# The sums of squares of a local-attention projection in a PSUM bank of their own

## The chip, the cores and the metric

The kernel runs on one core of a Trainium2 chip. The core has a matmul engine (TensorE, "PE" in the profile, with weight loads listed as PEld), a vector engine (VectorE, DVE), a scalar engine (ScalarE, ACT), a general engine (GpSimd, POOL) and SyncE (SP), which issues the DMAs here. Each engine works through its own list of instructions in order, and waits on semaphores for the others. Matmul results are written to PSUM, which the kernel divides into eight banks of 128 x 512 fp32 numbers. The metric is the time of one execution on the device in microseconds (us).

## The reference, cut to what matters

Two blocks, L0 and L1, follow each other on a batch of 2 with 2048 tokens of 128 numbers. Each block has an attention part and a "local model". The change lies in the local models: L0's has 6 layers with 16 heads and a window of 32, L1's has 2 layers with 8 heads and a window of 64; a head has 64 numbers. L1's linear attention lies between them. A layer of a local model computes this:

```python
def shift_token(x):
    t1, t2 = jnp.split(x, 2, axis=-1)
    t2 = jnp.pad(t2, ((0, 0), (1, 0), (0, 0)))[:, :-1]
    return jnp.concatenate([t1, t2], axis=-1)

def l2norm(t):
    return t / jnp.clip(jnp.linalg.norm(t, axis=-1, keepdims=True), 1e-12)

h = shift_token(x)
q, k, v = jnp.split(h @ wqkv, 3, axis=-1)      # then split into heads
q = l2norm(q) * qs
k = l2norm(k) * ksc
q, k = rotary_xpos(q, k)                       # t*cos*scale + rotate_half(t)*sin*scale; k with 1/scale
o = local_attention(q, k, v)                   # each window of queries sees its own and the last window
x = x + o @ wo
h = shift_token(x)
h = (h - mean) / sqrt(var + 1e-05) * lg + lb
a, g = jnp.split(h @ w1 + b1, 2, axis=-1)
x = x + (a * gelu(g)) @ w2 + b2
```

The norm inside `l2norm` needs, for each token and head, the sum of 64 squares and its reciprocal root.

## The kernel before, in words

A first stage computes L0's attention. Then `local_models` runs both local models in one loop. It works on tiles of 128 tokens: 16 tiles for each of 2 batches and each layer, 192 tiles for the first model and 64 for the second. The loop is a software pipeline: in one round it projects tile j, turns the rows of tile j-1 and computes its values, and does scores, softmax, mixing and the output of still earlier tiles.

For one tile these steps matter:

- `project` (L871 to L904) multiplies 128 tokens by 1024 columns of the weights into `pq` (`ps_qk`), a wide pair of PSUM banks. ACT squares it to `sq` (L873). DVE multiplies it by two tables, for the rotation, into `r` (L881) and `t` (L886), and POOL adds the two (L892). The first model needs two such units for a tile, half 0 and half 1, for its 2048 columns of queries and keys; the second needs one.
- After the last unit, DVE sums the squares by head (L897) and takes the reciprocal root in nine small steps (`rsqrt_quick`, L167 to L180). Their scratch, at most 128 columns, lies in `pq`. POOL multiplies `r` by the root (L904).
- `turn` (L936) transposes `r`, four transposes to a bank, into queries and keys (four banks a tile in the first model, two in the second).
- `values` (L955) projects the values, `scores` opens with a mask matmul (L986, two per tile, called M here) and adds the products (L995); DVE takes the maximum (L1003) and subtracts it (L1005), ACT takes the exponential (L1012), DVE sums (L1019), POOL scales (L1021).
- `keys_first_` (L1030) transposes the weights, `mix` (L1048) multiplies them with the values, `project_out` (L1065) projects the result (`ps_y`), and DVE adds it to the state (L1071).
- `feed_forward` works on four tiles at a time. Its steps (L1096, L1105 to L1110, L1128, L1131, L1148 twice, L1173) are put into a list, and each round of the loop takes two of them.

PSUM is split into two pools: `wide` hands out two pairs of banks in turn, for scores, projections and parts of the linear attention; `bank` hands out four single banks in turn, for everything else. An allocation waits until the last reader of the bank that it gets is done.

The order of instructions on each engine is not the order of the text. A scheduler in the build works from estimated durations and decides it, and with it which bank an allocation gets, and so which wait stands before which instruction. Once built, the order is fixed.

Of the kernel before, what the change touches and what calls it, by code (L numbers as in the profile page):

```python
# [72 lines left out]
def tile_kernel(ctx: ExitStack, tc: tile.TileContext, a: dict, out: bass.AP):  # L73
# [27 lines left out]
    def bc(ap, shape):  # L101
        return ap.to_broadcast(list(shape))
# [59 lines left out]
    def rsqrt_quick(scr, n, pool):  # L162

        x, xm, h, p = scr
        nc.vector.tensor_scalar(xm, x, 1e-24, None, ALU.max)  # L167
        y = pool.tile([128, n], F32, name="rq_g")
        nc.vector.tensor_scalar(
            y.bitcast(I32), xm.bitcast(I32), -0.5, RSQ_SEED, ALU.mult, ALU.add  # L170
        )
        nc.vector.tensor_tensor(p, xm, y, ALU.mult)
        hs_ = pool.tile([128, n], F32, name="rq_h")
        nc.vector.tensor_tensor(hs_, p, y, ALU.mult)
        nc.vector.tensor_tensor(h, p, y, ALU.mult)
        nc.vector.scalar_tensor_tensor(p, h, RSQ_A[0], hs_, ALU.add, ALU.mult)
        for c in RSQ_A[1:3]:
            nc.vector.scalar_tensor_tensor(p, p, c, hs_, ALU.add, ALU.mult)
        r = pool.tile([128, n], F32, name="rq_y", bufs=2)
        nc.vector.scalar_tensor_tensor(r, p, RSQ_A[3], y, ALU.add, ALU.mult)  # L180
        return r
# [526 lines left out]
    def local_models(mA, mB, hs0):  # L708
# [3 lines left out]
        wk = ctx2.enter_context(tc.tile_pool(name="f_k", bufs=1))  # L712
# [4 lines left out]
        def wide(name):  # L717

            return psA.tile([128, 1024], F32, tag="A", name=f"ps_{name}")

        def bank(name):
            return psT.tile([128, 512], F32, tag="T", name=f"ps_{name}")
# [139 lines left out]
        def project(i, u):  # L862
            g, b, t = tiles[i]
            m, _ = layers[g]
            H, units = m.H, m.units
            tb = tabs[g, t]
            hw = hs[0][:, b, t * 128:(t + 1) * 128]
            pq = wide("qk")
            for j in range(2):
                js = slice(512 * j, 512 * j + 512)  # L870
                nc.tensor.matmul(pq[:, js], lhsT=hw, rhs=wts[g, u][:, js], start=True, stop=True)  # L871
            sq = wk.tile([128, 1024], F32, name="sq", bufs=2)
            nc.scalar.activation(sq, pq, AF.Square)  # L873
            r = wk.tile([128, 1024], F32, name=f"r{u}", bufs=2)
            t2 = wk.tile([128, 1024], F32, name="t2", bufs=1)
            same = units[u][0][0] == units[u][1][0]
            for e in range(1) if same else range(2):
                s = units[u][e][0]
                hn = 16 if same else 8
                es = slice(512 * e, 512 * e + 64 * hn)  # L880
                nc.vector.tensor_tensor(  # L881
                    r[:, es].rearrange("p (h d) -> p h d", d=DH),
                    pq[:, es].rearrange("p (h d) -> p h d", d=DH),
                    bc(tb[:, 0, s].unsqueeze(1), (128, hn, DH)), ALU.mult,
                )
                nc.vector.tensor_tensor(  # L886
                    t2[:, es].rearrange("p (h s d) -> p h s d", s=2, d=32),
                    pq[:, es].rearrange("p (h s d) -> p h s d", s=2, d=32)[:, :, ::-1, :],
                    bc(tb[:, 1, s].rearrange("p (s d) -> p s d", s=2).unsqueeze(1),
                       (128, hn, 2, 32)), ALU.mult,  # L890
                )
            nc.gpsimd.tensor_tensor(r, r, t2, ALU.add)  # L892
            st[i]["r", u], st[i]["sq", u] = r, sq
            if u == len(units) - 1:

                for v in range(len(units)):
                    nc.vector.tensor_reduce(  # L897
                        pq[:, 16 * v:16 * v + 16],
                        st[i].pop(("sq", v)).rearrange("p (h d) -> p h d", d=DH), AX.X, ALU.add,
                    )  # L900
                y = rsqrt_quick([pq[:, k * 32:k * 32 + 2 * H] for k in range(4)], 2 * H, wk)
                for v in range(len(units)):
                    rv = st[i]["r", v].rearrange("p (h d) -> p h d", d=DH)
                    nc.gpsimd.tensor_tensor(  # L904
                        rv, rv, bc(y[:, 16 * v:16 * v + 16].unsqueeze(2), (128, 16, DH)), ALU.mult
                    )
# [554 lines left out]
        for i in range(-3, n):  # L1461
# [7 lines left out]
            if j < n:  # L1469
                g, b, t = tiles[j]  # L1470
                jj = j % per
                nu = len(layers[g][0].units)
                more = g < last
                if g == second and t % 4 == 0:
                    while (b, t // 4) not in ready:
                        lstep()
                if nu == 2:
                    project(j, 0)
                if more and jj == 4:
                    load_proj(g + 1, 0)  # L1480
                if more and jj == 6 and g + 1 == second:
                    models[1].consts()
                if jj == 6 and g == second - 1:
                    linear_consts()
                if more and jj == 8:
                    factors(g + 1)
                    if 2 == 2:
                        load_out(g + 1)
                if more and jj == 18:
                    load_ff(g + 1)  # L1490
                if more and jj == 22:
                    fold_ff(g + 1)
                if nu == 2 and more and jj == per - 1:
                    load_proj(g + 1, 1)
                lstep()
# [5 lines left out]
            if j < n:  # L1501
                project(j, nu - 1)
                if nu == 2 and more and jj == per - 1 and g + 1 < second:
                    load_proj(g + 1, 2)
                if nu == 1 and more and jj == per - 1:
                    load_proj(g + 1, 1)
                if b == B - 1 and j + 1 < n:
                    tables(*tiles[j + 1][::2])
# [93 lines left out]
```

## Time and profile before

| quantity | value |
|---|---|
| time, median of 3 runs | 4991.75 us (4983.2 to 4993.75) |
| the profiled execution's own time | 4992.08 us |
| its span, first to last instruction | 4990.3 us |
| busy: PE, DVE, ACT, POOL | 4522.4, 3949.9, 2641.9, 2783.4 us |
| granted TensorE clock, mean | 0.956 of full |
| first projection of the first model | at 572.7 us |
| first projection of the second model | at 3976.6 us |
| PE busy, 1500 to 1750 us (first model) | 240.2 of 250 us, clock 0.99 |
| PE busy, 4500 to 4750 us (second model) | 220.3 of 250 us, clock 0.95 |

A line of a group or of the timeline names the engine, the line of the kernel, the operation, the tile that is written and those that are read. "idle before <- X" is the time for which the engine stood still before the instruction, and what released it. The end of a matmul is modelled, so that neighbouring matmuls can overlap by some 0.15 us in the timeline.

### The profile page before, as it was taken

Reading aid. Unit: us, or ns where it says so; the run is one execution under the profiler, and the core shown is the slowest. Engines: PE = TensorE matmul, PEld = TensorE weight load, DVE = VectorE, ACT = ScalarE, POOL = GpSimd, SP = SyncE. Lnnn points to the kernel's source line nnn. Section 1 sums busy time; section 2 is a strip of 40 time slices with the busy share of each in tenths; the row PEclk is TensorE's granted clock in tenths of the full one; section 3 lists DMA queues with packets and bytes.
Section 4 is the critical chain, followed back from the end, with each engine's and each line's share of the span. In section 5 each row is a group of like instructions: output and inputs, shape, how many; then the busy total and the mean of one; then the engine's idle time right before and its main releaser. Section 6 shows DMA issues by size and latency. Waiting matters only on the chain.

```text
span 4990.3 us, 166474 instructions
## 1 busy us (share of the span) xinstructions
PE 4522.4 (91%) x73028; PEld 3080.9 (62%) x73058; DVE 3949.9 (79%) x6840; ACT 2641.9 (53%) x4207; POOL 2783.4 (56%) x1666
## 2 busy tenths in 40 slices
PE   5667799999999999999999999999999998989887
PEld 3445566666666666666666666666666665555554
DVE  6993488888887888888888888888877777778776
ACT  3223355555555555555555555555555555555554
POOL 3332366666666666666666666666555544455552
PEclk8778899999999999999999999999999999999999
DMA  2000222223222322232222322232221211111111
GB/s 77 1 1 25 84 68 67 64 72 78 68 64 63 84 71 64 64 82 72 65 70 61 80 67 64 66 82 68 55 58 49 63 45 40 40 46 40 50 48 41
DMA packets 222468, 295.32 MB, mean 59 GB/s; under 512 B 75656, under 2 KB 95408, under 8 KB 221744
## 3 DMA queue, kind: packets, MB, share of 16 engines
q1 hardware_dynamic: 221744, 284.67, 22.1%
q8 instruction: 576, 9.44, 0.8%
q14 instruction: 148, 1.21, 0.1%
HBM read 40.98 MB, written 10.75 MB: 10 GB/s over the span
## 4 chain that ended last, share of the span: by engine, by line
PE 47%; DVE 25%; ACT 7%; POOL 6%; issue 4%; DMA 1%; SPq 0%; POOLq 0%; DVEq 0%; ACTq 0%
PE ps_qk L871 11%; PE ps_o L1048 5%; PE ps_f L1148 5%; DVE ps_qk L897 5%; PE ps_v L955 5%; DVE t L886 5%; PE ps_turn L936 4%; POOL r L892 4%; PE ps_y L1065 4%; PE ps_s L995 3%; DVE r L881 3%; PE ps_fy L1173 3%; DVE rs L1019 2%; ACT sq L873 2%; PE ps_pT L1030 2%
## 5 line engine op out<-in xcount | busy, mean ns | idle before, releaser
L892 POOL TENSOR_TENSOR r<-r,t 128x1024 f32<-128x1024 f32 x448 | 1061.8, 2370 | 926.2 <-DVE t L886 814.6
L904 POOL TENSOR_TENSOR r<-r,rq_y 128x1024 f32<-128x1024 f32 x448 | 844.5, 1903 | 521.8 <-DVE rq_y L180 498.9
L873 ACT ACTIVATE sq<-ps_qk 128x1024 f32<-128x1024 f32 x448 | 461.0, 1029 | 1091.5 <-PE ps_qk L871 1026.4
L871 PE MATMUL ps_qk<-wp,hs 128*128 128x512 f32 x1792 | 894.9, 622 | 110.0 <-DVE rq_y L180 82.6
L881 DVE TENSOR_TENSOR r<-ps_qk,tb 128x1024 f32<-128x1024 f32 (+1 forms) x512 | 550.9, 1076 | 215.2 <-ACT sq L873 200.9
L1048 PEld LDWEIGHTS ps_o<-pT,v 64*64 64x64 f32 (+1 forms) x26624 | 479.4, 136 | 309.5 <-ACT pT L1031 162.4
L886 DVE TENSOR_TENSOR t<-ps_qk,tb 128x1024 f32<-128x1024 f32 (+1 forms) x512 | 554.5, 1083 | 145.5 <-POOL r L892 145.0
L1021 POOL TENSOR_TENSOR sm<-sm,rs 128x1024 f32<-128x1024 f32 x256 | 487.9, 1906 | 255.5 <-DVE rs L1020 172.7
L1048 PE MATMUL ps_o<-pT,v 64*64 64x32 f32 (+1 forms) x26624 | 532.1, 221 | 36.5 <-ACT pT L1031 19.9
L897 DVE TENSOR_REDUCE ps_qk<-sq 128x16 f32<-128x1024 f32 x448 | 549.2, 1226 | 12.0
L871 PEld LDWEIGHTS ps_qk<-wp,hs 128*128 128x128 f32 x1792 | 310.5, 193 | 367.6 <-issue 236.5
L936 PEld LDWEIGHTS ps_turn<-ident,r 128*128 128x128 f32 x3584 | 413.1, 144 | 157.0 <-issue 98.2
L936 PE MATMUL ps_turn<-ident,r 128*128 128x128 f32 x3584 | 450.1, 278 | 40.4 <-POOL r L904 36.9
L955 PE MATMUL ps_v<-wp,hs 128*128 128x512 f32 x896 | 482.2, 640 | 1.1 <-ACT oT L1054 0.8
L1065 PEld LDWEIGHTS ps_y<-oT,wo 128*128 128x128 f32 x3584 | 432.1, 193 | 48.3 <-issue 43.0
L1065 PE MATMUL ps_y<-oT,wo 128*128 128x128 f32 x3584 | 448.5, 277 | 1.7 <-ACT oT L1054 1.5
L1003 DVE TENSOR_REDUCE mx<-ps_s 128x16 f32<-128x1024 f32 (+1 forms) x256 | 312.5, 1221 | 101.5 <-PE ps_s L995 99.6
L1054 ACT COPY oT<-ps_o 128x512 f32<-128x512 f32 x448 | 243.8, 588 | 276.0 <-PE ps_o L1048 275.2
L995 PE MATMUL ps_s<-kT,qT 64*32 64x64 f32 (+1 forms) x26624 | 384.1, 231 | 0.3 <-issue 0.3
L995 PEld LDWEIGHTS ps_s<-kT,qT 64*32 64x32 f32 (+1 forms) x26624 | 331.0, 108 | 63.1 <-issue 49.4
L1148 PE MATMUL ps_f<-fx,w 128*128 128x512 f32 (+1 forms) x768 | 364.5, 612 | 2.3 <-DVE fx L1131 1.9
L1019 DVE TENSOR_REDUCE rs<-sm 128x16 f32<-128x1024 f32 (+1 forms) x256 | 310.6, 1213 | 62.3 <-ACT sm L1012 61.2
(265 smaller groups left out, 6860.3 us busy)
## 6 DMA issues: line engine op xcount, KB each, us to landing
v<-vn SPq DMA_DIRECT2D x1276, 128.0 KB
v<-vn SPq DMA_DIRECT2D x744, 64.0 KB
v<-vn SPq DMA_DIRECT2D x64, 256.0 KB
wp<-in_L_ffn_Wqkv SPq DMA_DIRECT2D x20, 512.0 KB
xD<-xb SPq DMA_DIRECT2D x24, 256.0 KB
xb<-xD SPq DMA_DIRECT2D x24, 256.0 KB
cs<-in_cos SPq DMA_DIRECT2D x128, 32.0 KB
cs<-in_sin SPq DMA_DIRECT2D x128, 32.0 KB
```

The lines of the kernel that those rows point to most:

```text
L871: nc.tensor.matmul(pq[:, js], lhsT=hw, rhs=wts[g, u][:, js], start=True, stop=True)
L881: nc.vector.tensor_tensor(r[:, es].rearrange("p (h d) -> p h d", d=DH), pq[:, es].rearrange("p (h d) -> p h d", d=DH), bc(tb[:, 0, s].unsq ...
L886: nc.vector.tensor_tensor(t2[:, es].rearrange("p (h s d) -> p h s d", s=2, d=32), pq[:, es].rearrange("p (h s d) -> p h s d", s=2, d=32)[: ...
L892: nc.gpsimd.tensor_tensor(r, r, t2, ALU.add)
L897: nc.vector.tensor_reduce(pq[:, 16 * v:16 * v + 16], st[i].pop(("sq", v)).rearrange("p (h d) -> p h d", d=DH), AX.X, ALU.add,)
L904: nc.gpsimd.tensor_tensor(rv, rv, bc(y[:, 16 * v:16 * v + 16].unsqueeze(2), (128, 16, DH)), ALU.mult)
L936: nc.tensor.transpose(p[:, c * 128:(c + 1) * 128], r[:, cs], ident)
L955: nc.tensor.matmul(p, lhsT=hw, rhs=wv, start=True, stop=True)
L995: nc.tensor.matmul(sp[W * w:W * w + W, c0:c0 + 2 * W], lhsT=qT[64 * q:64 * q + 64, cc, W * w:W * w + W], rhs=kT[64 * q:64 * q + 64, cc, W ...
L1048: nc.tensor.matmul(po[s][64 * q:64 * q + 64, 128 * c + W * w:128 * c + W * w + W], lhsT=v2[kp, w, co:co + 64], rhs=pT[kp, q, c, W * w:W * ...
L1065: nc.tensor.matmul(py[:, 0:128], lhsT=wts[g, "o"][:, c * NO + s, :], rhs=oT[:, s, c, :], start=(c + s == 0), stop=(c == 3 and s == NO - 1),)
L1148: nc.tensor.matmul(ps_[c][0:sz], lhsT=wts[g, "w1"][:, o:o + sz], rhs=S["x"], start=True, stop=True,)
```

## The change

After the last unit of a projection, a single bank `ss` is taken from the pool of four. The sums of squares and the scratch of the root lie there, not in the wide pair `pq`. The computation is the same.

```diff
             if u == len(units) - 1:
 
+                ss = bank("ss")
                 for v in range(len(units)):
                     nc.vector.tensor_reduce(
-                        pq[:, 16 * v:16 * v + 16],
+                        ss[:, 16 * v:16 * v + 16],
                         st[i].pop(("sq", v)).rearrange("p (h d) -> p h d", d=DH), AX.X, ALU.add,
                     )
-                y = rsqrt_quick([pq[:, k * 32:k * 32 + 2 * H] for k in range(4)], 2 * H, wk)
+                y = rsqrt_quick([ss[:, k * 32:k * 32 + 2 * H] for k in range(4)], 2 * H, wk)
                 for v in range(len(units)):
```

## The prediction

> **What bounds the kernel now.** I read the page's table of busy time first, then TensorE's waits, then one tile's timeline, engine by engine, and last the granted clock around one stall. TensorE (PE) is the busiest engine:
>
> ```profile
> PE 4522.4 (91%) x73028; PEld 3080.9 (62%) x73058; DVE 3949.9 (79%) x6840; ACT 2641.9 (53%) x4207; POOL 2783.4 (56%) x1666
> ```
>
> The waits of PE (who waited for whom, us in total, times, longest) name what the change touches: the next projection (L871) waits for the last root step (L180), which still holds the wide pair.
>
> ```profile
> PE ps_qk L871 <- DVE rq_y L180: 82.6, 82, 3.7
> ...
> PE ps_qk L871 <- DVE sm L1005: 19.2, 30, 3.4
> ...
> PE ps_s L986 <- DVE t L886: 2.6, 2, 1.4
> ```
>
> The timeline of one tile of the first model (start, us, count, idle before) shows why: PE has little slack, and VectorE (DVE) works in series through the whole tile.
>
> ```profile
> 1713.75 1.98 PE L871 MATMUL ps_qk<-wp,hs 128*128 128x512 f32 x4 [0.62 <-DVE rq_y L180]
> 1715.57 1.04 PE L1030 MATMUL ps_pT<-ident,sm 128*128 128x128 f32 x8
> 1716.44 1.88 PE L871 MATMUL ps_qk<-wp,hs 128*128 128x512 f32 x4
> 1718.27 0.30 PE L1048 MATMUL ps_o<-pT,v 64*64 64x32 f32 x4
> ...
> 1722.51 1.91 PE L936 MATMUL ps_turn<-ident,r 128*128 128x128 f32 x16
> 1724.25 0.60 PE L1128 MATMUL ps_r<-ident,frt 128*128 128x128 f32 x4
> 1724.69 1.95 PE L1065 MATMUL ps_y<-oT,wo 128*128 128x128 f32 x16
> 1726.57 0.39 PE L986 MATMUL ps_s<-L_maskb,pick 64*128 64x512 bf16 x2
> 1726.89 1.77 PE L995 MATMUL ps_s<-kT,qT 64*32 64x64 f32 x128
> 1729.44 1.13 PE L871 MATMUL ps_qk<-wp,hs 128*128 128x512 f32 x2 [0.78 <-DVE rq_y L180]
> ```
>
> ```profile
> 1719.10 1.22 DVE L886 TENSOR_TENSOR t<-ps_qk,tb 128x1024 f32<-128x1024 f32 x1
> ...
> 1722.85 1.23 DVE L886 TENSOR_TENSOR t<-ps_qk,tb 128x1024 f32<-128x1024 f32 x1 [1.30 <-POOL r L892]
> 1724.11 2.49 DVE L897 TENSOR_REDUCE ps_qk<-sq 128x16 f32<-128x1024 f32 x2
> ...
> 1729.20 0.19 DVE L180 SCALAR_TENSOR_TENSOR rq_y<-ps_qk,rq_g 128x32 f32<-128x32 f32 x1
> ```
>
> The first half's second product (L886) ends at 1720.32 and the last root step at 1729.40. At 1722.5 PE turns the *previous* tile's rows, seven us before this tile's root is done; nothing makes it wait. That freedom is at stake.
>
> **The change part by part.**
>
> *Instructions.* None is added or removed: the same two sums (L897, 1.23 us each) and nine steps (about 0.2 us) run on DVE on a PSUM bank of another pool. Between no dearer and 0.05 us a step either way (their rows in two widths differ by no more), 11 x 0.05 x 192 = 106 us at most; I take 0, since shape and memory are unchanged. No DMA and no POOL work is added; SP's and POOL's queues follow their producers.
>
> *What goes.* The pair is free after L886 instead of L180, so the 82.6 us of PE waits go, if nothing else is late.
>
> *What comes, first.* The scheduler rebuilds PE's order. Per tile of the first model, read from the built programs:
>
> ```
> before: scores, qk half 0, pT, qk half 1, o, v, turn, y, mask of next scores
> after:  scores, qk half 0, pT, qk half 1, mask of next scores, o, v, turn, y
> ```
>
> (Line numbers are the old kernel's; from L896 on the new one's are one higher.) The mask matmul (L986) opens the next scores in the pair that half 0 held, so it waits for half 0's L886. In the rows above PE is past half 1 at 1718.27 and L886 ends at 1720.32: 2.05 us of idle. Behind it stand o, v, turn, y and the next scores.
>
> *What comes, second.* The four single banks rotate. With the sums taking one in each tile, 12 are handed out per tile instead of 11 (apart from the feed-forward's, FF), and the fourth after the sums waits for L180 of the *same* tile. In the built program that is the third of the turn's four banks in six tiles of eight, and the last FF matmul in a seventh. Behind it: half the turn, y, the scores, the next projection, and through the scores all of DVE's next tile. From L886's end (time 0) PE needs mask 0.3, o and v 3.9 (2028.7 to 2032.6 in a tile that does not split them), half the turn 0.9: 5.1 us. DVE reaches L180 at 9.08 less what stands after it in the new order (L1131 0.58, two L1071 0.49): 8.0, and 8.2 with bubbles it covered. So PE idles 3.1 us.
>
> *The new tile.* From one first-half L886 to the next: L180 at 8.2 (gate), then half the turn 0.9, y 1.85 and the scores 1.45 (4.2), then from the scores' end to the next L886 6.5 (1713.75 to 1720.32 is 6.57, of which the projection overlaps the scores' tail by 0.07). Sum 18.9 us for a tile without FF work; before, 15.2 to 15.7. Eight tiles repeat with two FF blocks. FF work behind the gated turn adds fully; FF work ahead of the mask fills PE's idle there and changes the head: in the timeline L886 ends 5.8 after the scores with L1148 ahead of it (DVE then does it before L1019) and 5.4 with L1173. The gate is 9.0 where L1105 and L1108 (0.8) stand among the sums, and 9.3 where ACT's gelu holds the second half's square back (that half's L886 came 4.8 us after the first's instead of 3.8). So the second row is 8.2 + 4.2 + 2.6 + 5.8, the third 9.3 + 4.2 + 2.6 + 6.5, and so on. In the last two rows PE's own work decides: 7.2 ahead of the mask and 11.6 or 11.3 behind it. Before is measured from L886 to L886, 1772.92 to 1908.33:
>
> | FF before mask / after turn | before | after |
> |---|---|---|
> | none | 15.2 | 18.9 |
> | L1128 / L1148 (2.6) | 16.1 | 20.8 |
> | L1148 / L1173 (2.6) | 19.5 | 22.5 |
> | none | 15.2 | 19.0 |
> | L1096 (DVE 0.8 in the sums) | 16.8 | 19.7 |
> | none / L1128 (0.4) | 15.7 | 19.4 |
> | L1148 / L1148, its last gated | 18.5 | 18.8 |
> | L1173 / L1096, not gated | 18.4 | 18.5 |
> | sum | 135.4 | 157.6 |
>
> That is +22 us per eight. 22 of 24 groups: +488; the last two also carry the linear attention, which fills the gaps; half: +22. Together +510.
>
> *Second model (64 tiles).* One projection per tile, and y (L1065) or an FF matmul at its place waits for L180. From the scores' end: maximum and subtraction 2.5, exponential 1.1, square 1.05, four half products 2.5, sum 1.2, steps 1.8: 10.2; PE is at y after 6.2. Then y 0.9 and scores 1.05: 12.2 us. Eight tiles with some 14 us of FF work outside the gap make 112; before, eight tiles took 103.8 and 109.2 (4564.82 to 4668.59 to 4777.83). +6 a group, 8 groups: +45.
>
> *The clock.* Idle PE time has a second price, in the granted clock (columns: stretch, length, PE, PEld, DVE, ACT, POOL busy, PEclk):
>
> ```profile
> 1981.40:1984.80 3.40, 1.62 (x117) 1.43 (x97) 3.13 (x13) 0.00 (x0) 0.90 (x2) 0.99 0.47 121
> 1984.80:1988.20 3.40, 3.40 (x5) 1.23 (x5) 2.11 (x2) 0.00 (x0) 3.40 (x2) 0.50 0.00 0
> ```
>
> A stretch with 1.78 us idle is followed by 3.4 us at half clock; the projection in it took 3.68 instead of 1.98 us. A gap of 3.1 us leaves 1.78 or more in one such stretch in (3.1+3.4-2x1.78)/3.4 = 0.86 of phases, the 2.05 us gap in 0.56. After the earlier gap the slow stretch falls on work with 3 us of slack, and shortens the later gap until that one is harmless. So 0.44 x 0.86 = 0.38 times at most 1.7 us: 0.6 us a tile on some 190 tiles: +115. Bounds: 0, and 0.86 x 1.7 x 190 = 278.
>
> The Trainium skill (TensorE: Matmul & The Clock Gate, HAM oscillation) sets its rule at idle gaps over about 3.4 us. By that, neither gap would throttle and the sum would be 5547; the row, where a 1.78 us stall was enough, goes first.
>
> *Sum.* The profiled execution took 4992.1 us (span 4990.3 and 1.8 around it), 0.3 above the median 4991.75, so it stands for it. 4992 + 510 + 45 + 115 = 5662, rounded to **5660**. That already contains the 82.6 us that go.
>
> **The rivals.**
> - *Faster.* The old waits go and the new ones are met in time: 4992 - 83 - 9 (half of the waits for L1005) = 4900. It needs L180 within 5.1 us of the first L886. For: 82 waits are real. Against: the rows say 8.2, and the first half's t, POOL's add (2.37) and the second half's t are in series.
> - *Only the mask wait costs.* If the bank wait is met (same point, 5.1 us), a plain tile is 6.5 + 0.3 + 3.9 + 1.75 + 1.85 + 1.45 = 15.8, and the eight sum to 15.8 + 18.3 + 19.0 + 15.8 + 15.8 + 16.2 + 19.0 + 17.3 = 137.2, +1.8 x 24 = +45: 5035. For it: a mask wait is two products deep only. Against: the same 8.2.
> - *Clock collapses.* Every gap throttles and the slow stretches lengthen DVE's chain too: 4992 + 555 + 278 and the second model's share (1.3 x 64): 5910.
> - *No change.* PE trades one DVE wait for another of equal length: 4990. Against: the new gates fall 5 us before the work they wait for, the old ones under 1 us on average.
>
> **How the numbers follow.** Forecast 0.76, only the mask 0.10, clock collapse 0.08, no change 0.02, faster 0.04. About 0.2% is what a measurement of this kernel can tell from no change. Slower: 0.76 + 0.10 + 0.08 = 0.94; same 0.02; faster 0.04. The forecast's own range: below, 5547 without clock loss, less 190 tiles x 0.75 us should the chain overlap better than I see: 5400; above, the clock's bound and half of the 106 us of the DVE steps: 5662 + 163 + 53 = 5880. I give 5400 to 5900, which leaves out mask-only, faster and no change (0.16).
>
> **What would show it.** Right: waits L871 <- L180 gone; the turn (L937 after) waiting for L180 with some 400 to 600 us, the mask (L987) for L886 with 250 to 400; PE's busy share near 80%, DVE's near 70%; plain tiles of 18.5 to 20 us; granted clock 0.87 to 0.93 in the first model's layers. Wrong: L180 ends before the third turn bank is due, or tiles stay at 16 us.

## The result, and the profile after

The changed kernel takes 5745.5 us (median of 4 runs, 5728.1 to 5756.0) against 4987.5 us before (4 runs): a ratio of 1.152, 95% interval 1.148 to 1.155. The profiled execution took 5755.99 us (span 5754.2, mean granted clock 0.919) against 4992.08 us (0.956).

The busy times on the page of the changed kernel, then its list of TensorE's waits (who waited for whom: us in total, times, longest); lines from L896 on are one higher than before:

```profile
PE 4727.8 (82%) x73028; PEld 3234.4 (56%) x73058; DVE 3983.0 (69%) x6840; ACT 2667.2 (46%) x4217; POOL 2776.0 (48%) x1666
```

```profile
PE ps_turn L937 <- DVE rq_y L180: 319.4, 121, 5.6
PE ps_s L987 <- DVE t L886: 179.7, 108, 2.7
PE ps_y L1066 <- DVE rq_y L180: 60.2, 15, 4.4
...
PE ps_qk L871 <- DVE t L886: 11.5, 5, 3.2
```

The projection's wait for L180 is gone (82.6 us before). In its place the turn, y and the mask matmul wait, 559 us in these three lines; TensorE went from 91% busy to 82%.

One tile of the first model, TensorE's timeline and then two lines of VectorE's (start, us, count, idle before):

```profile
2175.88 1.98 PE L871 MATMUL ps_qk<-wp,hs 128*128 128x512 f32 x4
...
2179.01 1.88 PE L871 MATMUL ps_qk<-wp,hs 128*128 128x512 f32 x4
2182.51 0.39 PE L987 MATMUL ps_s<-L_maskb,pick 64*128 64x512 bf16 x2 [1.62 <-DVE t L886]
...
2186.65 1.04 PE L937 MATMUL ps_turn<-ident,r 128*128 128x128 f32 x8
2190.71 1.07 PE L937 MATMUL ps_turn<-ident,r 128*128 128x128 f32 x8 [3.02 <-DVE rq_y L180]
2191.61 4.44 PE L1149 MATMUL ps_f<-fx,w 128*128 128x512 f32 x6
...
2201.00 2.74 PE L1149 MATMUL ps_f<-fx,w 128*128 128x512 f32 x6
```

```profile
2181.24 1.22 DVE L886 TENSOR_TENSOR t<-ps_qk,tb 128x1024 f32<-128x1024 f32 x1
...
2190.38 0.19 DVE L180 SCALAR_TENSOR_TENSOR rq_y<-ps_ss,rq_g 128x32 f32<-128x32 f32 x1
```

After the second projection half the mask matmul stands idle for 1.62 us; the first eight transposes run; the other eight stand for 3.02 us until L180, the last reader of the bank that they are to get. L886 ends at 2182.46 and L180 at 2190.57: 8.1 us later. Note also the six feed-forward matmuls (L1149) right behind the gap, 4.44 us for what takes 2.74 us a little later: the granted clock is at half from 2191.8 to 2195.2.

Where the time came from, by stretches from the starts of L180 (the first of the first model, the first of the second, the last):

| kernel | median of runs | first model | second model |
|---|---|---|---|
| before (profiled 4992) | 4987 | 3392.5 | 932.6 |
| after (profiled 5756) | 5746 | 3959.0 | 1115.0 |
| difference, profiled | +764 | +566 | +182 |

The remaining 15 us lie outside the two stretches. Over the second to the 21st of the first model's 24 groups, eight tiles took 162.7 us on average instead of 137.4.

### The profile page after: what moved, and what is told of

Same layout as the page of the kernel before. It is cut to its first block, busy times and chain, and to the rows that moved or that the text cites. A ratio compares the mean times of both kernels' runs of the same rounds, so it can differ in the third digit from the quotient of the medians.

```text
span 5754.2 us, 166430 instructions
## 1 busy us (share of the span) xinstructions
PE 4727.8 (82%) x73028; PEld 3234.4 (56%) x73058; DVE 3983.0 (69%) x6840; ACT 2667.2 (46%) x4217; POOL 2776.0 (48%) x1666
## 3 DMA queue, kind: packets, MB, share of 16 engines
q1 hardware_dynamic: 221744, 284.67, 19.1%
## 4 chain that ended last, share of the span: by engine, by line
PE 43%; DVE 33%; ACT 7%; POOL 4%; issue 3%; DMA 0%; POOLq 0%; DVEq 0%; ACTq 0%; SPq 0%
PE ps_y L1066 8%; DVE t L886 6%; PE ps_qk L871 6%; PE ps_s L996 6%; DVE ps_ss L898 6%; PE ps_turn L937 5%; DVE r L881 5%; PE ps_f L1149 4%; POOL r L892 4%; DVE rs L1020 4%; PE ps_v L956 3%; PE ps_o L1049 3%; PE ps_fy L1174 3%; ACT sq L873 2%; DVE sm L1006 2%
## 5 line engine op out<-in xcount | busy, mean ns | idle before, releaser
L871 PE MATMUL ps_qk<-wp,hs 128*128 128x512 f32 x1792 | 876.1, 610 | 18.5 <-DVE t L886 11.5
L937 PE MATMUL ps_turn<-ident,r 128*128 128x128 f32 x3584 | 501.2, 288 | 323.3 <-DVE rq_y L180 319.4
L937 PEld LDWEIGHTS ps_turn<-ident,r 128*128 128x128 f32 x3584 | 436.7, 150 | 496.8 <-issue 236.1
L886 DVE TENSOR_TENSOR t<-ps_qk,tb 128x1024 f32<-128x1024 f32 (+1 forms) x512 | 553.3, 1081 | 145.2 <-POOL r L892 145.0
L1066 PE MATMUL ps_y<-oT,wo 128*128 128x128 f32 x3584 | 516.4, 303 | 61.6 <-DVE rq_y L180 60.2
L1066 PEld LDWEIGHTS ps_y<-oT,wo 128*128 128x128 f32 x3584 | 498.0, 218 | 114.4 <-DVE rq_y L180 63.7
L898 DVE TENSOR_REDUCE ps_ss<-sq 128x16 f32<-128x1024 f32 x448 | 546.2, 1219 | 8.6 <-ACT g L1387 2.3
L956 PE MATMUL ps_v<-wp,hs 128*128 128x512 f32 x896 | 513.5, 693 | 18.6 <-DVE rq_y L180 14.9
L1072 DVE TENSOR_TENSOR hs<-ps_y,hs 64x128 f32<-64x128 f32 x512 | 147.9, 289 | 524.5 <-PE ps_y L1066 519.5
L871 PEld LDWEIGHTS ps_qk<-wp,hs 128*128 128x128 f32 x1792 | 305.6, 191 | 259.8 <-issue 224.5
L1149 PE MATMUL ps_f<-fx,w 128*128 128x512 f32 (+1 forms) x768 | 382.5, 637 | 32.7 <-DVE rq_y L180 30.6
L942 ACT COPY kT<-ps_turn 128x512 f32<-128x512 f32 x448 | 251.0, 602 | 319.1 <-PE ps_turn L937 318.3
```

Of the source, the lines that this page charges most:

```text
L886: nc.vector.tensor_tensor(t2[:, es].rearrange("p (h s d) -> p h s d", s=2, d=32), pq[:, es].rearrange("p (h s d) -> p h s d", s=2, d=32)[: ...
L898: nc.vector.tensor_reduce(ss[:, 16 * v:16 * v + 16], st[i].pop(("sq", v)).rearrange("p (h d) -> p h d", d=DH), AX.X, ALU.add,)
L937: nc.tensor.transpose(p[:, c * 128:(c + 1) * 128], r[:, cs], ident)
L956: nc.tensor.matmul(p, lhsT=hw, rhs=wv, start=True, stop=True)
L1066: nc.tensor.matmul(py[:, 0:128], lhsT=wts[g, "o"][:, c * NO + s, :], rhs=oT[:, s, c, :], start=(c + s == 0), stop=(c == 3 and s == NO - 1),)
L1149: nc.tensor.matmul(ps_[c][0:sz], lhsT=wts[g, "w1"][:, o:o + sz], rhs=S["x"], start=True, stop=True,)
```

## The experiments

Two things are told apart first. The change releases the pair of banks earlier, and it puts a tile with a late last reader into the ring of four. Theory (ring): only the second costs. Rival (early release): the earlier projections disturb what followed. After that the terms of the sum are tested: what a gate costs, what half clock costs, and what the early release is worth. Line numbers shift by a few between the kernels; the names of the tiles identify the lines. "The stretch" of a model is the one of the table above, always of the profiled execution; a model's stage is nearly the same, from its first projection to the next model's, or to the last. A ratio is to the kernel before, measured alongside, with its 95% interval.

### The pair held, the ring as changed

```diff
                 y = rsqrt_quick([ss[:, k * 32:k * 32 + 2 * H] for k in range(4)], 2 * H, wk)
+                hd = wk.tile([128, 1], F32, name="hd")
+                nc.vector.tensor_tensor(hd, pq[:, 0:1], y[:, 0:1], ALU.add)
```

> As the changed kernel, with the sums in a bank of the ring, but one small VectorE addition after L180 reads the wide pair, so the pair is held as long as in the kernel before. Theory (ring): nothing is won back: 5700 to 5850 us, the turn waits some 320 us for L180 as in the changed kernel. Rival (early release): with the old release the old time returns, 4990 to 5060 us.

Measured: 5749.3 us, ratio 1.154 [1.152, 1.156]; stretches 3965.7 and 1119.1. TensorE's waits in it:

```profile
PE ps_turn L939 <- DVE rq_y L180: 330.4, 128, 4.7
PE ps_s L989 <- DVE t L886: 182.6, 108, 2.4
...
PE ps_qk L871 <- DVE hd L904: 2.6, 3, 1.9
```

Nothing comes back. The built order is that of the changed kernel too, with the mask matmul right behind the projection. So neither the early release nor the pair has a part in the loss; the bank in the ring has all of it.

### The pair released, no sums in the ring

Two ways: a tile of SBUF, and a PSUM bank of its own at the price of one bank of the ring.

```diff
-    ones = const.tile([128, 128], F32, name="ones")
-    nc.vector.memset(ones, 1.0)
...
-                ss = bank("ss")
+                ss = wk.tile([128, 128], F32, name="ss")
```

> Sums and scratch lie in a tile of SBUF (a constant that nothing reads makes room): the wide pair is still free after L886, but no bank of the ring of four is taken. Theory (ring): the whole loss comes from the wait of a fourth allocation for the same tile's L180, so it goes, and so do the 82.6 us of waits of the projection: 4900 us if nothing is late next, 4990 if TensorE's or VectorE's own work takes their place; TensorE keeps the old order, with the mask matmul last. Rival (early release): the loss comes from the pair being free earlier, which changes what meets what: 5500 to 5750 us.

```diff
-        psT = ctx2.enter_context(tc.tile_pool(name="f_psT", bufs=4, space=PSUM))
+        psT = ctx2.enter_context(tc.tile_pool(name="f_psT", bufs=3, space=PSUM))
+        psQ = ctx2.enter_context(tc.tile_pool(name="f_psQ", bufs=1, space=PSUM))
...
-                ss = bank("ss")
+                ss = psQ.tile([128, 512], F32, tag="Q", name="ps_ss")
```

> Sums and scratch in a PSUM bank of their own that nothing else takes; the ring of the others has three banks instead of four. No allocation waits for L180 any more, so theory (ring gate) has the 750 us go; instead each of 11 allocations per tile waits for the reader three back instead of four back, ACT's copies for the most part: 4950 to 5200 us, the loss by three banks alone. Rival (a ring with fewer free banks per tile is what costs, through whatever reader): 5500 us or more.

Measured: sums_in_sbuf 4983.3 us, 0.9995 [0.9985, 1.0005]; own_bank 4981.8 us, 0.9995 [0.9984, 1.0005]. Both are at the old time, although both release the pair early, and own_bank does it with a ring of three. The ring theory holds: what costs is not how many banks there are but who must read one last. In both the mask matmul is back behind y, in most tiles; so the scheduler had moved it on account of the bank in the ring, which the prediction had not said.

The 82.6 us that the old wait was worth did not appear either. TensorE's waits in sums_in_sbuf (before: L871 for L1005 19.2 us, L936 for L904 36.9, L1048 for L1031 19.9):

```profile
PE ps_qk L869 <- DVE sm L1004: 59.2, 53, 3.3
PE ps_turn L935 <- POOL r L903: 43.7, 22, 4.0
...
PE ps_o L1047 <- ACT pT L1030: 39.7, 43, 5.1
```

About 67 of the 82.6 us turn up in these three lines: the projection now waits for the subtraction that still reads the scores in the pair it is to get, and later work waits for ACT and POOL.

sums_in_sbuf has a price of its own. From its timeline, VectorE and POOL:

```profile
1719.54 2.37 POOL L890 TENSOR_TENSOR r<-r,t 128x1024 f32<-128x1024 f32 x1
1721.27 0.67 DVE L165 TENSOR_SCALAR ss<-ss 128x32 f32<-128x32 f32 x1
...
1735.84 2.36 POOL L890 TENSOR_TENSOR r<-r,t 128x1024 f32<-128x1024 f32 x1 [0.82 <-DVE t L884]
1736.85 1.39 DVE L165 TENSOR_SCALAR ss<-ss 128x32 f32<-128x32 f32 x1
```

The first root step, 0.198 us on average in PSUM, ends where POOL's addition ends (1721.94 and 1721.91; 1738.24 and 1738.20), 0.773 us on average. Over the whole trace 191 of the 256 first steps take over 0.3 us, and 190 of these end within 0.12 us of a POOL instruction that was running when they began. In the kernel before, with the sums in PSUM, 162 of the 256 lie wholly inside a POOL instruction, and none takes over 0.2 us. The next run asked whether the slow steps had eaten the gain.

```diff
+        if two:
+            nc.vector.scalar_tensor_tensor(xm, x, 1e-24, x, ALU.max, ALU.max)
+        else:
+            nc.vector.tensor_scalar(xm, x, 1e-24, None, ALU.max)
...
+            nc.vector.scalar_tensor_tensor(
+                y.bitcast(I32), xm.bitcast(I32), -0.5, bc(seed, (128, n)), ALU.mult, ALU.add
+            )
```

> As sums_in_sbuf, but the first two root steps take a second tensor input (the sums once more, and a constant), so that they are of the form of the later steps, which took 0.19 us there. In sums_in_sbuf the first step took 0.77 instead of 0.20 us on average, and where I looked its end fell on the end of POOL's addition (L892), the second 0.28 to 0.52 instead of 0.19. Theory (the slow steps ate what the early release wins): VectorE's busy time falls from 4112 to 3950 us or less and the time to 4900 to 4940 us, below both kernels. Rival (nothing was to be won: the projection's wait only became one for L1005 and for POOL's rows, since TensorE has work for 96% of the first model's time): 4965 to 4990 us.

Measured: 4973.7 us, 0.9976 [0.9966, 0.9986], inside the rival's range. But the edit did not do what it was for, as VectorE's groups of it show (busy, mean ns of one):

```profile
L168 DVE SCALAR_TENSOR_TENSOR ss<-ss 128x32 f32<-128x32 f32 x192 | 150.1, 782 | 5.0
```

Still 782 ns: the other form waits for POOL as well, so this run does not test the theory. The Trainium skill (SBUF — State Buffer, Who interferes with whom) has the rule: a VectorE instruction in a two-port mode, or with two SBUF inputs against a GpSimd instruction that reads SBUF, shares a port pair with GpSimd, and whichever comes second stands until the first is done. The two ends above agree with it, and by it the edit was bound to fail.

### What a gate costs: an earlier, a later and a shorter one

```diff
-                ss = bank("ss")
+                ss, s2 = bank("ss"), bank("s2")
...
-                y = rsqrt_quick([ss[:, k * 32:k * 32 + 2 * H] for k in range(4)], 2 * H, wk)
+                y = rsqrt_quick([(s2 if k else ss)[:, k * 32:k * 32 + 2 * H] for k in range(4)], 2 * H, wk)
```

> As the changed kernel, but the scratch of the root takes a second bank of the ring, so the wait for L180 stands earlier in TensorE's order: ahead of the second half of the values and the whole turn instead of ahead of half the turn (first model), and ahead of half the turn instead of y (second model). Theory (the gate adds what stands behind it): half of the values 0.43 and half a turn 0.9 more behind the gate, 1.3 us on some 170 tiles, and 0.45 on 64: 5900 to 6050 us. Rival (a gap costs the same wherever it stands, as the idle time itself or its effect on the clock is the price): 5700 to 5800 us.

Measured: 6603.6 us, 1.3255 [1.3235, 1.3274]; stretches 4731.5 and 1200.9. The loss doubles, far beyond both. TensorE's timeline in it shows another mechanism:

```profile
2194.57 1.88 PE L871 MATMUL ps_qk<-wp,hs 128*128 128x512 f32 x4
2196.38 0.39 PE L987 MATMUL ps_s<-L_maskb,pick 64*128 64x512 bf16 x2
2203.13 2.05 PE L871 MATMUL ps_qk<-wp,hs 128*128 128x512 f32 x2 [6.36 <-DVE t L886]
```

The scheduler now put the mask matmul ahead of the second projection half. With the next scores in one pair, the second half must take the pair of the first half and waits for its products: 964.5 us in all. TensorE's work at half clock in the first model's stage rose as well, to 1417 us from 399 in the changed kernel. So this run does not price the gate's place; it shows how far one more late bank carries through the order.

```diff
-        nc.vector.tensor_scalar(xm, x, 1e-24, None, ALU.max)
+        for _ in range(5):
+            nc.vector.tensor_scalar(xm, x, 1e-24, None, ALU.max)
```

> As the changed kernel, but the first root step is made five times (the same result), which is 0.8 us more VectorE work per tile ahead of L180. It also shifts what the scheduler hands out meanwhile: by the built order, of eight tiles of the first model two then wait for L180 ahead of y, three ahead of a feed-forward matmul behind the whole turn, three not at all before the next round, where the changed kernel has six that wait in the middle of the turn and one ahead of its last feed-forward matmul. Theory (a gate costs L180's lateness plus what stands behind it): +0.8 and -0.9 us cancel on five tiles, and three are free: 5600 to 5760 us in spite of the longer chain. Rival (VectorE's chain alone sets the tile, wherever the gate stands): +0.8 us on some 230 tiles, 5900 to 5950 us.

Measured: 5798.7 us, 1.164 [1.161, 1.166]. That is between the two, and the stretches say why: the first model takes 3916.7 us, 42 less than in the changed kernel, in spite of 0.8 us more VectorE work per tile. There the place of the gate counts, as the theory has it: in the first model's stage the turn waits 16 us for L180 instead of 285, and y (90 us) and feed-forward matmuls (130 us) wait in its place. The second model, where the gates stand where they stood, takes 1198.4, 83 more. Four steps of 0.18 us on 64 tiles are 46 us. TensorE's work at half clock there rose from 214 to 297 us, which is up to 41 us more, so the longer gap seems to cost twice.

```diff
-        for c in RSQ_A[1:3]:
+        for c in RSQ_A[1:1]:
```

> As the changed kernel, with two of the nine root steps left out (so the roots are not those of the reference): L180 ends 2 x 0.2 us earlier in every tile, and the order of the built program stays nearly the same. Theory (L180 sets the end of the gated tiles): 0.39 us less on some 155 tiles of the first model and 0.36 on 64 of the second, 5650 to 5690 us. Rival (what costs is the order of TensorE's work, the wait for L886 or the clock): 5730 to 5760 us.

Measured: 5697.4 us (5667.0 to 5712.2, 6 runs), 1.1425 [1.1397, 1.1452]; stretches 3911.8 and 1083.0. The direction is the theory's, and the rival's range is left, but the theory's is missed by 7 us too: the gain is 48 us by the medians, against some 80 forecast. (By the stretches it is 79, but they compare the fastest of these six runs with the slowest of the changed kernel's four.) L180 sets the end of the gated tiles; by how much is known to some 30 us.

```diff
                 ss = bank("ss")
+                sc = wk.tile([128, 128], F32, name="sc")
...
-                y = rsqrt_quick([ss[:, k * 32:k * 32 + 2 * H] for k in range(4)], 2 * H, wk)
+                y = rsqrt_quick([(sc if k else ss)[:, k * 32:k * 32 + 2 * H] for k in range(4)], 2 * H, wk)
```

> As the changed kernel, but only the sums lie in the bank of the ring: the first root step (L167) writes to SBUF, and the other eight stay there. The bank is free after L167, 8 x 0.2 = 1.6 to 1.8 us ahead of L180. In the built order TensorE's sequence is that of the changed kernel, but the fourth allocation after the sums now is the second half of the values, so the gate stands ahead of that and of the whole turn (first model), and ahead of half the turn instead of y (second model). Theory (a gate costs its lateness plus all that stands behind it): 1.8 us earlier, 1.35 more behind it, 0.45 us less on some 155 tiles; 1.6 earlier and 0.45 more, 1.15 less on 64: about 5600 us, 5540 to 5650. Rival (only the lateness counts, wherever the gate stands): 1.7 us less on some 220 tiles, 5370 us.

Measured: 5861.8 us, 1.175 [1.172, 1.178]; stretches 4100.2 and 1090.2. Both expectations miss: the second model is 25 us shorter (74 forecast), the first 141 us longer. The bank is free 1.7 us earlier and the kernel is slower: the wait has moved ahead of the values and the whole turn. TensorE's waits, two lines of its timeline, and two of VectorE's groups:

```profile
PE ps_v L955 <- DVE sc L165: 284.0, 118, 4.8
PE ps_s L986 <- DVE t L884: 178.9, 107, 2.4
PE ps_turn L936 <- DVE sc L165: 157.3, 76, 3.2
```

```profile
2183.17 0.67 PE L1048 MATMUL ps_o<-pT,v 64*64 64x32 f32 x33 [1.31 <-issue]
2183.77 3.67 PE L955 MATMUL ps_v<-wp,hs 128*128 128x512 f32 x4
```

```profile
L167 DVE TENSOR_SCALAR rq_g<-sc 128x32 int32<-128x32 int32 x192 | 92.5, 482 | 6.1
L167 DVE TENSOR_SCALAR rq_g<-sc 128x16 int32<-128x16 int32 x64 | 74.2, 1159 | 2.0
```

The values take 3.67 us there instead of 1.98: half clock. In the first model's stage TensorE's work at half clock is 665 us against 399 in the changed kernel, up to 133 us of loss, which could be most of the 141. But the run changes a second thing: the root steps now work in SBUF, and the second of them takes 482 ns instead of 190 in the first model and 1159 instead of 172 in the second. VectorE is busy 158 us longer in all. So this run does not price the gate's place by itself, and the 49 us that the second model stays short of its forecast may be these slower steps.

### What half clock costs

```diff
-                for c in range(4):
+                for c in [0, 1, 2, 3] * (4 if W == 64 else 1):
```

> As the changed kernel, but in the second model each transpose of the turn is made four times (the same values to the same place), 24 more of 0.11 us = 2.6 us per tile, which fill most of the gap of 3.4 to 4.4 us ahead of the output projection. Theory (the clock after a gap is part of the second model's loss): y and the scores run at full clock, the second model's 1116 us from first to last projection become 985 to 1060, the time 5620 to 5690 us. Rival (only the wait itself costs): TensorE's busy time rises by some 165 us, the time stays within 20 us of the changed kernel's 5746, or is longer.

Measured: 5734.0 us, 1.152 [1.150, 1.153], 12 us below the changed kernel: by the whole time, the rival's case. By groups of eight tiles of the second model it is not. In the four whole groups without linear attention beside them, eight tiles take 129.8, 129.7, 132.2 and 132.9 us in the changed kernel and 120.8, 120.5, 122.3 and 126.1 here. In the first three, where other work stands beside them, they take 168.2, 166.5 and 142.6 there, 188.7, 176.1 and 146.8 here: the filler costs its own time where no gap is left for it. The timelines show the mechanism, first the changed kernel (TensorE and VectorE's last root step), then this one:

```profile
5255.39 1.83 PE L996 MATMUL ps_s<-kT,qT 64*64 64x128 f32 x32
...
5262.26 1.04 PE L937 MATMUL ps_turn<-ident,r 128*128 128x128 f32 x8
5267.63 2.07 PE L1066 MATMUL ps_y<-oT,wo 128*128 128x128 f32 x8 [4.33 <-DVE rq_y L180]
5269.63 1.99 PE L996 MATMUL ps_s<-kT,qT 64*64 64x128 f32 x32
```

```profile
5267.40 0.17 DVE L180 SCALAR_TENSOR_TENSOR rq_y<-ps_ss,rq_g 128x16 f32<-128x16 f32 x1
```

```profile
5315.49 3.66 PE L937 MATMUL ps_turn<-ident,r 128*128 128x128 f32 x32
5319.91 1.16 PE L1066 MATMUL ps_y<-oT,wo 128*128 128x128 f32 x8 [0.77 <-DVE rq_y L180]
5321.00 1.10 PE L996 MATMUL ps_s<-kT,qT 64*64 64x128 f32 x32
```

More work in the gap, and the tile is shorter: y and the scores take 2.26 us instead of 4.06. The clock over the second model's later part (from 4900 us in the one, 4850 in the other; columns as in the prediction's table of stretches, the clock third from the end):

```profile
4900.00:5670.20 770.20, 589.83 (x4940) 393.12 (x4929) 517.84 (x1057) 344.33 (x514) 318.18 (x203) 0.89 0.14 38
```

```profile
4850.00:5640.10 790.10, 699.62 (x6407) 501.93 (x6403) 554.15 (x1128) 380.89 (x557) 340.98 (x216) 0.98 0.14 40
```

From one L180 to the next, a tile without feed-forward work takes 14.1 to 14.2 us in the changed kernel and 12.6 here. So half clock is worth some 9 us (7 to 10) of the 26 (23 to 30) by which these groups of eight became longer.

```diff
-                for c in range(4):
+                for c in [0, 1, 2, 3] * (3 if W == 32 and u == 0 and i % 8 in (0, 1, 4, 5, 6, 7) else 1):
```

> As the changed kernel, but in six of eight tiles of the first model, those that wait for L180 in the middle of the turn, the transposes of the first two banks are made three times (the same values to the same place): 16 more of 0.11 us = 1.75 us in the gap of 3 us, which then is 1.3 us. Theory (half clock after the gaps is part of the first model's loss): half-clock work of TensorE there falls from 399 us to 200 or less, the feed-forward matmuls behind the gate take 2.74 instead of 4.44 us, and the time falls by 60 to 130 us: 5615 to 5685. Rival (half clock falls on work that has slack): the time stays at 5746, give or take 15.

Measured: 5772.3 us, 1.157 [1.156, 1.159], 27 us more than the changed kernel: a miss. The turn's wait for L180 halved (319 to 149 us) and the feed-forward matmuls behind the gate took 2.74 us again in the tile below, but TensorE's work at half clock only fell from 399 to 303 us, and eight tiles took 163.1 us over the same 20 groups, where the changed kernel has 162.7. In TensorE's timeline the slow stretch stands elsewhere:

```profile
2173.84 3.78 PE L956 MATMUL ps_v<-wp,hs 128*128 128x512 f32 x4
2177.42 4.10 PE L937 MATMUL ps_turn<-ident,r 128*128 128x128 f32 x32
2181.35 2.74 PE L1149 MATMUL ps_f<-fx,w 128*128 128x512 f32 x6
```

With a second gap left in the tile (the mask's), half clock moved to the values and the turn in this tile. What the first model loses to the clock is so not shown by a run; it is at most half of the 302 us by which its half-clock work grew (97 to 399).

### The mask brought forward without a gate

```diff
+        def masks(i):
...
+            if 0 <= i + 2 < n:
+                masks(i + 2)
             if i >= 0:
                 mix(i)
```

The mask matmul of `scores` moves into `masks`; the rest is own_bank.

> As own_bank (no wait for L180), with the mask matmul brought forward: asked for ahead of the mixing, it stands after two thirds of the mixing in four or five tiles of eight, some 1.2 us later than in the changed kernel, and there would wait 0.8 us for L886. Theory (TensorE has work for 96% of the time, so idle time in it counts in full): 0.8 us on some 100 to 120 tiles, 5060 to 5080 us. Rival (the wait takes the place of other short waits of the same tile): 4970 to 5000 us.

Measured: 4989.4 us, 1.0007 [0.9996, 1.0018]. The wait did not arise (`own_bank` has 2.3 us in the same line):

```profile
PE ps_s L987 <- DVE t L887: 8.6, 30, 2.0
```

In most tiles the mask matmul stands up to 1.2 us later here than in the changed kernel, so these do not settle its wait in full. But in 37 of the 150 tiles between 800 and 3400 us it stands right behind the projection, its place in the changed kernel, and it waits in none of them: TensorE is there 1.6 us after the end of L886 (median), where in the changed kernel it is there 1.6 us before it. That speaks for reading the wait as a result of the gate, which makes the scores and so VectorE's next products late.

### A version that beats both

```diff
-                ss = bank("ss")
+                if len(units) == 2:
+                    ss = wk.tile([128, 128], F32, name="ss")
+                else:
+                    if "ss" not in K:
+                        K["ss"] = bank("ss")
+                    ss = K["ss"]
```

> The pair is free after L886 and nothing in the ring waits for L180, by another place for the sums in each model: in the first model a tile of SBUF as in sums_in_sbuf (the ring keeps its four banks), in the second one bank that is taken once and kept for all its tiles as in own_bank (the ring has three from then on). Theory (the two parts add): from the first to the last L180 of the models, sums_in_sbuf has 3373 us in the first against 3393 before, own_bank 917 in the second against 933; 35 us together, 4950 us, a ratio of 0.993. Rival (these differences are scatter between profiled executions): 4975 to 4990 us.

Measured: 4953.7 us, 0.9933 [0.9917, 0.9949]; stretches 3365.5 and 918.2. The two parts add as forecast. So the early release can be worth 35 us, with a place for the sums that suits each model. One place for both gained 2 us (sums_in_sbuf and own_bank; 10 with sbuf_two_inputs), since each won in one model and lost in the other: sums_in_sbuf has 19 us less in the first and 8 more in the second, own_bank 15 more and 16 less.

## Why the prediction was right, and where its terms were off

Sign and mechanism hold; 5660 was 86 us short of 5746, within the range. That it came so near is in part luck, since two misses of opposite sign were added up: by the stretches of the profiled execution the terms of the first model (510 + 115) were 59 us too high, and that of the second (45) was 137 us too low.

- *Instructions at 0.* The root steps of the first model take 0.19 to 0.21 us after, 0.19 to 0.20 before. VectorE's busy time rose by 33 us, inside the bound of 106.
- *What goes, 82.6 us.* The wait went, the time did not. With the gate away (sums_in_sbuf, own_bank) the total is unchanged within 0.1%; best_of_both gains 35 us. "If nothing else is late" failed: the subtraction, ACT and POOL are.
- *What comes first, the mask.* It stands where the built order put it and waits 1.7 us on average (2.05 forecast), but only 108 times. It was told as a cost of its own; pair_held and sums_in_sbuf show that its move follows from the ring.
- *What comes second, the ring.* In the tile shown L180 ends 8.1 us after L886 (8.2), TensorE is there at 5.2 (5.1), the gap is 3.02 us (3.1). pair_held, sums_in_sbuf and own_bank show it to be the cause of the whole loss.
- *The new tile.* From one first-half L886 to the next, averaged over the same 20 groups, the eight rows measure 19.1, 21.9, 23.5, 20.2, 20.1, 20.2, 19.0 and 18.6 us. Five are within 0.8 us of the forecast (18.9, 19.7, 19.4, 18.8 and 18.5); the second, third and fourth are 1.0 to 1.2 above it (20.8, 22.5 and 19.0). The second and third have feed-forward matmuls right behind the gate, and in the tile shown these ran at half clock (4.44 us for 2.74). With the clock's 0.6 us a tile the forecast was 27.0 more per eight tiles; it became 25.3. The first model's stretch grew by 566 us, against 510 + 115.
- *The clock, +115.* The first model's part is at most 151 us, and no run isolates it. The runs side with the prediction's row and not with the rule that it was set against: by the Trainium skill (TensorE: Matmul & The Clock Gate, HAM oscillation), whose rule is "no PE-idle gaps >~3.4µs", neither gap would have throttled, and 5547 would have come out. Here a gap of 3.02 us was followed by half clock, and the first model's stage has 102 stretches at half clock against 22 before. But one row was too little for a threshold. The trace of the changed kernel gives the granted clock in steps of 3.41 us. Of the full-clock steps between the first and the last projection, those with over 2.0 us of idle time were followed by half clock in 110 of 112 cases, those with 1.4 to 2.0 us in 37 of 126, those with less in 6 of 1062. So 1.78 us, which the prediction took as enough, is a borderline case; weighted with these counts its shares of phases, 0.86 and 0.56, come to some 0.8 and 0.5 (an estimate). The granted clock of 0.87 to 0.93 forecast for these layers was too low, it is 0.95: there were fewer gaps than tiles, 111 for the turn and 108 for the mask on 192 tiles.
- *The second model, +45.* This is the term that failed: +182. Mechanism and gate were right: in the tile shown with filled_second L180 ends 10.35 us after the scores (10.2) and TensorE is at y after 6.1 (6.2). But the clock was priced for the 190 tiles of the first model alone. The gap is longer here, mostly 3.4 to 4.4 us (half of the first model's are under 2.9), and y and the scores behind it took 4.06 us instead of the 1.95 in the sum. filled_second gives 9 of the 26 us per eight back and clears half clock nearly (0.89 to 0.98). Of the other 17, 6 were forecast. The rest is read from filled_second's trace and not shown by a run of its own: a plain tile takes 12.6 us there (12.2 in the sum), and eight tiles take 20 to 25 us more than eight plain ones, where the sum had 14 for the feed-forward work.
- *What would show it.* The turn's 319 us and the mask's 180 fall short of 400 to 600 and 250 to 400: in some tiles feed-forward work stands in the place of the gap. Busy shares (82% for 80, 69% for 70) hold.

## What to carry to other kernels

A tile that moves into a shared ring of buffers makes a later, unrelated allocation wait for its last reader: find which allocation that is, how late that reader ends, and what stands behind that wait on its engine. Count the built order's change as part of the edit, since a scheduler that sees the new wait moves other work, and pairs and rings then meet differently. A gap on TensorE has a second price in the clock of what follows it, so price it in every stage that has the gap, and take its threshold from many steps of the trace rather than from one row.

## What the runs showed of the hardware

- The first root step (32 columns on VectorE), moved from PSUM to SBUF, went from 0.198 to 0.773 us: 190 of 191 slow ones, in both models, ended with a POOL instruction that was running. In a form with a second tensor input it took 0.782.
- The granted clock of TensorE changed in steps of 3.41 us. After a full-clock step with over 2.0 us of idle time half clock followed in 110 of 112 cases, after one with under 1.4 us in 6 of 1062.
- Making TensorE do 24 needless transposes per tile, in a gap, shortened eight tiles from 129.8 to 120.8 us, with the granted clock of the stage up from 0.89 to 0.98.
